# Fourier stage, last part: spectra transposed for two units at a time, into two tiles used in turn

## Chip, cores and metric

The kernel runs on one core of one Trainium2 chip. The metric is the device time of one execution in microseconds (us). Three executions of the kernel before took 6373.64, 6377.86 and 6387.61 us; the median is 6377.86 us.

## The reference

The reference is a four-layer network over an image tensor of 4 x 64 x 64 x 128 floats. Each layer is a mixing part and a feed-forward part. The change lies in the mixing part of the third layer, a Fourier neural operator with attention, and there in its last part. Cut to what is computed in that part (`p` is the spectral convolution of the attention's output, whose half-spectrum the kernel holds on chip when the part begins):

```python
        p = _fno_layer(av, Pcw, Psw, H, W)
        a = _inorm(p + xa, attn_w, attn_b)
        an = _inorm(a, norm2_w, norm2_b)
        m = _fno_layer(an, m0cw, m0sw, H, W, inner_norm=True, act=True)
        m = _fno_layer(m, m1cw, m1sw, H, W, inner_norm=True, act=False)
        out = _inorm(m, mon_w, mon_b) + a
```

with `_fno_layer` being an inverse Fourier transform of a filtered spectrum plus a pointwise skip, `_inorm` a normalization over an image, and everything in float32.

## The kernel before

**Units.** The last part handles 16 units: four batches `b`, four groups `g` each. A unit is a generator, `group(b, g, pT)` at L2187, with 28 steps between its yields. It takes the half-spectrum of its 16 images, brings it back to the image (`inverse` at L2049, with the matmuls of L2200 and L2066), normalizes, transforms forward (`transform` at L2071, `spectra` at L2085), multiplies with the first filter on VectorE (`filtered` at L2094, instructions of L2101 and L2106), brings it back (`back` at L2111, matmuls of L2116), applies the activation (L2173), and repeats this with the second filter.

**Rounds.** Units are run as a software pipeline. In one round each active unit does two steps. Every fourth round a new unit enters, and a unit lives 14 rounds, so that three to four units are active in each. Within a round the units are taken in an order by their age. The order on each engine comes out of a scheduler that mostly keeps the order in which instructions are written, and brings forward what is ready when an engine would be idle.

**The spectra.** The half-spectrum lies in the SBUF tile `ph`, 128 x 2 x 64 x 66: the partitions are images of two batches, 64 rows each. The first inverse needs it with the 66 frequencies on partitions, in the tile `pT`. `groups()` at L2280 makes it for a whole batch when the batch's first unit is due: eight PSUM tiles `ptp` of 66 x 8 x 64, each filled by eight TensorE transposes with 64 partitions in (L2287) and each copied to `pT` by one ScalarE copy (L2288). `pT` has one buffer; a batch's four units read it. This falls at the start of rounds 0, 16, 32 and 48.

**PSUM banks.** The tiles of tag `pr` take turns in three PSUM banks: the `prf` of `transform`, the `pz` of `spectra`, the `pi` of `inverse`, and also the `ptp` of the transposes. `pf` has four banks and `pm` one. A `pr` bank comes free when ScalarE (`fr` at L2081, `ir` at L2059, `pT` at L2288) or VectorE (`w` at L2101, for `pz`) has read it.

**Warming.** `warm` at L2044 puts matmuls whose result is overwritten (L2047) ahead of some real ones, so that TensorE is busy there.

Where a new unit enters, TensorE's order is: the second half of `prf` of the unit that is in its seventh stage (L2079), the transposes if a batch begins (L2287), the new unit's `pi` (L2200), then warming and the back transform of the unit of stage 4 (L2047, L2116), then `pz` of the unit of stage 8 (L2090). ScalarE's order at that place is: the activation `m` and `fr` of the stage-7 unit, six of its `sk` (L2173), the `pT` copies if a batch begins, and the new unit's `ir`.

Of the kernel before, what the change touches and what calls it, by code (L numbers as in the profile page):

```python
# [10 lines left out]
F32 = mybir.dt.float32  # L11
# [1576 lines left out]
def stage_fourier(k, a):  # L1588
# [11 lines left out]
    nc, tc = k.nc, k.tc  # L1600
    with ExitStack() as octx:
# [55 lines left out]
        with ExitStack() as ctx:  # L1657
# [8 lines left out]
            with ExitStack() as ctx2:  # L1666
# [3 lines left out]
                ps = ctx2.enter_context(tc.tile_pool(name="fo_ps", bufs=2, space=PSUM))  # L1670
# [94 lines left out]
                for b in range(4):  # L1765
# [4 lines left out]
                    for g in range(8):  # L1770
# [5 lines left out]
                        for hf in range(2):  # L1776
                            pr = ps.tile([128, 2, 256], F32, tag="pr", name="pr")
# [70 lines left out]
            with ExitStack() as ctx2:  # L1848
                yp = ctx2.enter_context(tc.tile_pool(name="fo_y", bufs=3))
                ps = ctx2.enter_context(tc.tile_pool(name="fo_pss", bufs=2, space=PSUM))  # L1850
                for hg in range(4):
                    hs = slice(8 * hg, 8 * hg + 8)
                    acc = [ps.tile([128, 8, 64], F32, tag=f"acc{bp}", name=f"acc{bp}") for bp in range(2)]
                    for g in range(17):
                        n = 128 if g < 16 else 64
# [31 lines left out]
        ph = php.tile([128, 2, 64, 66], F32, tag="ph", name="ph")  # L1887
        with ExitStack() as ctx:
# [15 lines left out]
            with ExitStack() as ctx2:  # L1904
                sm = ctx2.enter_context(tc.tile_pool(name="fo_as", bufs=2))
                ps = ctx2.enter_context(tc.tile_pool(name="fo_psa", bufs=2, space=PSUM))
# [8 lines left out]
                for bp in range(2):  # L1915
                    for q in range(4):
                        pt = ps.tile([128, 4, 128], F32, tag="pt", name="pt")
# [7 lines left out]
                for bp in range(2):  # L1925
                    pt = ps.tile([128, 128], F32, tag="pt", name="pta")
# [20 lines left out]
            with ExitStack() as ctx2:  # L1947
# [4 lines left out]
                ps = ctx2.enter_context(tc.tile_pool(name="fo_psv", bufs=3, space=PSUM))  # L1952
# [20 lines left out]
                for q in range(16):  # L1973
                    acc = [ps.tile([128, 3, 132], F32, tag="acc", name=f"acc{bp}") for bp in range(2)]
                    for hp in range(16):
                        n = 2 * q + hp // 8
# [37 lines left out]
        with ExitStack() as ctx:  # L2014
            bp_ = ctx.enter_context(tc.tile_pool(name="fo_b", bufs=1))
            sm = ctx.enter_context(tc.tile_pool(name="fo_m", bufs=2))
            ps = ctx.enter_context(tc.tile_pool(name="fo_psm", bufs=3, space=PSUM))
            mw = []
            for i in range(2):
# [3 lines left out]
                for u in range(2):  # L2023
                    p, n = mc[:, 2 * u], mc[:, 2 * u + 1]
# [127 lines left out]
            def inv(d):  # L2152
                r = eight("r")
                nc.vector.reciprocal(r, d)
                return r
# [31 lines left out]
            def group(b, g, pT):  # L2187
# [7 lines left out]
                    nc.gpsimd.tensor_tensor(sk[:, h4], sk[:, h4], xa[:, h4], op=ALU.add)  # L2195

                def terms(out, h, j):
                    n0 = 16 * g + 8 * h + 2 * j
                    for a in range(2):
                        nc.tensor.matmul(  # L2200
                            out[64 * a : 64 * a + 64], pT[:, a, n0 : n0 + 2, :].rearrange("p n y -> p (n y)"), ra[:, a, :], start=True, stop=True
                        )

                pfs = yield from inverse(terms, dya)
                for h in range(2):
                    h4 = slice(4 * h, 4 * h + 4)
# [32 lines left out]
                r, q, c, bias = inv(d), eight("q"), eight("c"), eight("sh")  # L2239
# [4 lines left out]
                y = tile8("m", 4)  # L2244
# [19 lines left out]
                r, q = inv(d), eight("q")  # L2264
# [12 lines left out]
                yield  # L2277
                yield

            def groups():  # L2280
                for b in range(4):
                    pT = bp_.tile([66, 2, 64, 32], F32, tag="pT", name="pT")
                    rows = slice(64 * (b % 2), 64 * (b % 2) + 64)
                    for q in range(8):
                        pt = ps.tile([66, 8, 64], F32, tag="pr", name="ptp")
                        for j in range(8):
                            nc.tensor.transpose(pt[:, j, :], ph[rows, b // 2, 8 * q + j, :], k.ident[rows, rows])  # L2287
                        nc.scalar.copy(pT[:, q // 4, :, 8 * (q % 4) : 8 * (q % 4) + 8].rearrange("p n y -> p y n"), pt)  # L2288
                    for g in range(4):
                        yield group(b, g, pT)  # L2290

            waiting, active, rounds = groups(), [], 0
            while waiting is not None or active:
                n = next(waiting, None) if waiting is not None and rounds % 4 == 0 else None
                if n is not None:
                    active.insert(0, [n, 0])
                elif rounds % 4 == 0:
                    waiting = None
                active.sort(key=lambda a_: {13: 0, 7: 12}.get(a_[1], a_[1]))
                for _ in range(2):  # L2300
                    for a_ in active:
                        next(a_[0])
                for a_ in active:
                    a_[1] += 1
                active = [a_ for a_ in active if a_[1] < 14]
                rounds += 1
# [736 lines left out]
def body(nc, tc, x, out, parts):  # L3043
    with ExitStack() as ctx:
        k = Ctx(nc, tc, ctx)
        dram = ctx.enter_context(tc.tile_pool(name="x1", bufs=1, space=DRAM))
        x1 = dram.tile([4, 64, 64, 128], F32, tag="x1", name="x1")
        stage_deformable(k, x, x1, *parts["conv0"].values())
        k.load_x(x1, ctx)
        stage_expert_choice(k, *parts["ffn0"].values())  # L3050
        stage_triangle(k, *parts["conv1"].values())
        stage_recurrent(k, *parts["ffn1"].values())
        stage_fourier(k, {n[3:]: v for n, v in parts["conv2"].items()})
        stage_moe(k, *parts["ffn2"].values(), "L2")
        stage_pair_attention(k, *parts["conv3"].values())
        stage_moe(k, *parts["ffn3"].values(), "L3")
        k.store_x(out)
# [25 lines left out]
```

## Time and profile before

| | |
|---|---|
| median of three executions | 6377.86 us |
| profiled execution, its own time | 6364.91 us |
| its span | 6363.0 us |
| mean granted TensorE clock | 0.906 |
| PE busy over the span | 5519.0 us (87%) |
| DVE busy | 4620.7 us (73%) |
| ACT busy | 2911.1 us (46%) |
| the transposes L2287 | x256, first at 3240.8, last at 3702.7 us |
| the copies L2288 | x32, median 1076 ns |
| the matmuls L2200 | x512, first at 3250.8, last at 3818.4 us |

The table is read like this: the part in question runs from about 3240 to 3960 us of the span. PE is TensorE's matmul row, PEld its weight loads, DVE is VectorE, ACT is ScalarE, POOL is GpSimd. The granted clock is the share of full TensorE speed that the chip allowed; it changes within the part. A line such as L2200 is a line of the kernel before.

### The profile page before, as it was taken

Reading aid. Unit: us, or ns where it says so; the run is one execution under the profiler, and the core shown is the slowest. Engines: PE = TensorE matmul, PEld = TensorE weight load, DVE = VectorE, ACT = ScalarE, POOL = GpSimd, SP = SyncE. Lnnn points to the kernel's source line nnn. Section 1 sums busy time; section 2 is a strip of 40 time slices with the busy share of each in tenths; the row PEclk is TensorE's granted clock in tenths of the full one; section 3 lists DMA queues with packets and bytes.
Section 4 is the critical chain, followed back from the end, with each engine's and each line's share of the span. In section 5 each row is a group of like instructions: output and inputs, shape, how many; then the busy total and the mean of one; then the engine's idle time right before and its main releaser. Section 6 shows DMA issues by size and latency. Waiting matters only on the chain. (4 is left out here: it accounts for less than half of the span.)

```text
span 6363.0 us, 143766 instructions
## 1 busy us (share of the span) xinstructions
PE 5519.0 (87%) x57327; PEld 2980.4 (47%) x57327; DVE 4620.7 (73%) x9921; ACT 2911.1 (46%) x6599; POOL 2075.5 (33%) x1828
## 2 busy tenths in 40 slices
PE   8978888856688788988999987988998998989999
PEld 4446666644456564333455654335234253252233
DVE  7868777745377753868978888875866857858877
ACT  5635555533154332750145554755344353353375
POOL 0012222210001111007841111443645654636545
PEclk9988888987789899999998997997997988979999
DMA  6666888871500013039920000002111112111101
GB/s 171 178 183 203 244 244 241 248 228 37 176 1 1 2 39 84 11 106 190 182 59 12 13 11 6 1 7 62 37 51 44 40 40 53 39 53 43 32 20 33
DMA packets 714227, 545.15 MB, mean 86 GB/s; under 512 B 299872, under 2 KB 625000, under 8 KB 710216
## 3 DMA queue, kind: packets, MB, share of 16 engines
q1 hardware_dynamic: 671400, 495.22, 29.1%
q10 hardware_dynamic: 42144, 40.58, 2.0%
q8 instruction: 458, 7.50, 0.5%
q14 instruction: 225, 1.84, 0.1%
HBM read 366.25 MB, written 152.86 MB: 82 GB/s over the span
## 5 line engine op out<-in xcount | busy, mean ns | idle before, releaser
L2901 DVE TENSOR_TENSOR t<-S,q 128x1536 f32<-128x1536 f32 x512 | 893.5, 1754 | 165.1 <-PE S L2901 165.1
L2901 POOL TENSOR_TENSOR t<-t,q 128x512 f32<-128x512 f32 x512 | 652.0, 1273 | 509.1 <-ACT t L2901 504.3
L2901 ACT COPY t<-S 128x512 f32<-128x512 f32 x512 | 300.2, 586 | 836.4 <-PE S L2901 763.3
L2901 PE MATMUL S<-R,L 32*128 32x512 f32 x4096 | 611.8, 651 | 53.9 <-DMA R<-wd 42.0
L2901 PE MATMUL acc<-t,sum 128*32 128x512 f32 x4096 | 548.3, 608 | 0.6 <-DVE t L2901 0.5
L2567 PE MATMUL pe<-ew,yT 128*128 128x512 f32 x1024 | 490.7, 615 | 27.3 <-DVE xs L2573 24.8
L937 DVE COPY_PREDICATED band<-bit,band 128x384 f32<-128x384 int32 (+11 forms) x384 | 313.5, 928 | 168.0 <-ACT band L928 148.7
L918 PE MATMUL S<-kpad,qm 32*64 32x144 f32 (+3 forms) x8192 | 358.3, 399 | 70.8 <-ACT band L928 26.5
L2573 DVE SCALAR_TENSOR_TENSOR xs<-pe,gate,xs 128x128 f32<-128x128 f32 x1024 | 331.2, 344 | 96.6 <-PE pe L2567 81.7
L2901 PEld LDWEIGHTS S<-R,L 32*128 32x128 f32 x4096 | 178.7, 186 | 472.2 <-ACT t L2901 396.9
L1989 PE MATMUL acc<-w,attT 128*64 128x396 f32 x2048 | 347.9, 499 | 25.9 <-issue 15.1
L2576 ACT ACTIVATE sc<-pe,gate 128x128 f32<-128x128 f32 x1024 | 291.2, 379 | 161.6 <-PE pe L2567 139.8
L1985 DVE TENSOR_TENSOR w<-xp,e 128x1188 f32<-128x1188 f32 x256 | 335.9, 1385 | 33.2 <-ACT xp L1968 15.9
L918 PEld LDWEIGHTS S<-kpad,qm 32*64 32x64 f32 x8192 | 262.0, 149 | 125.8 <-issue 60.8
L1029 PE MATMUL pt<-ident,D 128*128 128x128 f32 x1536 | 259.5, 316 | 62.6 <-DMA D<-dd 45.7
L2567 PEld LDWEIGHTS pe<-ew,yT 128*128 128x128 f32 x1024 | 183.5, 194 | 267.7 <-issue 172.3
L1984 POOL TENSOR_TENSOR w<-xtl,e 128x396 f32<-128x396 f32 x256 | 260.7, 1035 | 117.1 <-DMA e<-ed 74.2
L1031 ACT COPY dt<-pt 128x512 f32<-128x512 f32 x384 | 204.2, 594 | 133.6 <-PE pt L1029 132.8
L2901 PEld LDWEIGHTS acc<-t,sum 128*32 128x32 f32 x4096 | 81.3, 108 | 392.2 <-issue 366.7
L1445 POOL TENSOR_TENSOR xs<-xs,zT 128x512 f32<-128x512 f32 x32 | 39.6, 1281 | 677.3 <-DVE zT L1444 676.8
L1989 PEld LDWEIGHTS acc<-w,attT 128*64 128x64 f32 x2048 | 158.2, 137 | 215.7 <-issue 145.3
L1029 PEld LDWEIGHTS pt<-ident,D 128*128 128x128 f32 x1536 | 212.8, 203 | 85.6 <-DMA D<-dd 58.5
(544 smaller groups left out, 11691.6 us busy)
## 6 DMA issues: line engine op xcount, KB each, us to landing
vb<-vd SPq DMA_DIRECT2D x272, 256.0 KB
e<-ed SPq DMA_DIRECT2D x64, 792.0 KB
D<-dd SPq DMA_DIRECT2D x128, 192.0 KB
D<-dd SPq DMA_DIRECT2D x128, 168.0 KB
D<-dd SPq DMA_DIRECT2D x128, 144.0 KB
w<-in_e_weight_dram ACTq DMA_DIRECT2D x16, 1024.0 KB
w<-in_e_weight_dram SPq DMA_DIRECT2D x16, 1024.0 KB
D<-dd SPq DMA_DIRECT2D x128, 120.0 KB
```

Source lines behind the costliest of these rows:

```text
L918: ins = nc.tensor.matmul(acc[g][64 * h : 64 * h + 64].rearrange("p (a s) c -> p a s c", a=3), qm[rows, h, m, :], keys, start=(m == 0), sto ...
L937: nc.vector.copy_predicated(flat[:, :, 0:n], bit[:, 0, :, i : i + 1].to_broadcast([128, 48, n]), flat[:, :, s : s + n])
L1029: ins = nc.tensor.transpose(pt[:, g, :], D[:, g, ty : ty + 382 : 3], k.ident)
L1031: nc.scalar.copy(dt, pt)
L1445: nc.gpsimd.tensor_tensor(k.xs[b][:, 4 * g : 4 * g + 4, :], k.xs[b][:, 4 * g : 4 * g + 4, :], s, op=ALU.add)
L1984: nc.gpsimd.tensor_tensor(w[:, 3:4], planes[q][:, 3:4], wide(1, [[132, 3], [1, 132]]), op=ALU.mult)
L1985: nc.vector.tensor_tensor(w[:, 0:3].rearrange("p b c m -> p b (c m)"), xp[:, q % 2], wide(3, [[1, 396]]), op=ALU.mult)
L1989: nc.tensor.matmul(acc[b // 2][64 * (b % 2) : 64 * (b % 2) + 64].rearrange("p c m -> p (c m)"), attT[:, b // 2, hp, 64 * (b % 2) : 64 * (b ...
L2567: nc.tensor.matmul(pe[h].rearrange("p e c -> p (e c)"), yT[:, 128 * t : 128 * t + 128], ew[:, 4 * h : 4 * h + 4, :].rearrange("p e c -> p ...
L2573: nc.vector.scalar_tensor_tensor(xt, pe[0][:, e, :], gate[:, t, e : e + 1], xt, op0=ALU.mult, op1=ALU.add)
L2576: nc.scalar.activation(sc[:, e, j, :], pe[1][:, e, :], AF.Copy, scale=gate[:, t, 4 + e : 5 + e])
L2901: last[engine] = f(*args, **kw)
```

## The change

The transposes are no longer made for a batch of 64 partitions when it begins, but for a pair of units, of 32 partitions. `turned(p, a)` makes half of pair `p`: for one half `a` of the rows it fills two PSUM tiles of 66 x 16 x 32, by 16 transposes of 32 partitions each, and copies each with one ScalarE copy. Both halves of the first pair are made before the loop. From then on one call stands at the end of every fourth round, 14 in all, so that a pair is ready before its first unit enters. `pT` is half as large, 66 x 2 x 32 x 32, and has two buffers in turn. The units read it with an offset for the unit's place in the pair. The list of waiting units is replaced by a count, and the order within a round is given by a table `rank`.

```diff
                 def terms(out, h, j):
-                    n0 = 16 * g + 8 * h + 2 * j
+                    n0 = 16 * (g % 2) + 8 * h + 2 * j
...
-            def groups():
-                for b in range(4):
-                    pT = bp_.tile([66, 2, 64, 32], F32, tag="pT", name="pT")
-                    rows = slice(64 * (b % 2), 64 * (b % 2) + 64)
-                    for q in range(8):
-                        pt = ps.tile([66, 8, 64], F32, tag="pr", name="ptp")
-                        for j in range(8):
-                            nc.tensor.transpose(pt[:, j, :], ph[rows, b // 2, 8 * q + j, :], k.ident[rows, rows])
-                        nc.scalar.copy(pT[:, q // 4, :, 8 * (q % 4) : 8 * (q % 4) + 8].rearrange("p n y -> p y n"), pt)
-                    for g in range(4):
-                        yield group(b, g, pT)
-
-            waiting, active, rounds = groups(), [], 0
-            while waiting is not None or active:
-                n = next(waiting, None) if waiting is not None and rounds % 4 == 0 else None
-                if n is not None:
-                    active.insert(0, [n, 0])
-                elif rounds % 4 == 0:
-                    waiting = None
-                active.sort(key=lambda a_: {13: 0, 7: 12}.get(a_[1], a_[1]))
+            pTs = {}
+
+            def turned(p, a):
+
+                if a == 0:
+                    pTs[p] = bp_.tile([66, 2, 32, 32], F32, tag="pT", name="pT", bufs=2)
+                b, r0 = p // 2, 64 * (p // 2 % 2) + 32 * (p % 2)
+                rows = slice(r0, r0 + 32)
+                for y0 in (0, 16):
+                    pt = ps.tile([66, 16, 32], F32, tag="pr", name="ptp")
+                    for j in range(16):
+                        nc.tensor.transpose(pt[:, j, :], ph[rows, b // 2, 32 * a + y0 + j, :], k.ident[rows, rows])
+                    nc.scalar.copy(pTs[p][:, a, :, y0 : y0 + 16].rearrange("p n y -> p y n"), pt)
+
+            for a in range(2):
+                turned(0, a)
+            rank = {n: i for of in ((0, 4, 8, 12), (13, 1, 5, 9), (2, 6, 10), (3, 11, 7)) for i, n in enumerate(of)}
+            active, rounds = [], 0
+            while rounds < 64 or active:
+                n = rounds // 4
+                if rounds % 4 == 0 and n < 16:
+                    active.append([group(n // 4, n % 4, pTs[n // 2]), 0])
+                active.sort(key=lambda a_: rank[a_[1]])
                 for _ in range(2):
                     for a_ in active:
                         next(a_[0])
+                if rounds % 4 == 3 and n < 14:
+                    turned(n // 2 + 1, n % 2)
                 for a_ in active:
                     a_[1] += 1
                 active = [a_ for a_ in active if a_[1] < 14]
```

## The prediction

> **What bounds it now.** The chain of waits that ended last lies in the last stages and says nothing of this part, so I read the part itself: first where the transposes run (instructions of L2287, L2288), then the timelines of TensorE and ScalarE at a place where a batch begins and at one where only a unit enters, then the granted clock there. Where only a unit enters, TensorE shows this (start, length, engine, line, operation, out<-in, count, and the idle time before it with its releaser):
>
> ```profile
> 3449.97 1.64 PE L2079 MATMUL prf<-dyp,m 128*128 128x128 f32 x8 [0.50 <-ACT m L2173]
> 3453.14 1.16 PE L2079 MATMUL prf<-dyp,m 128*128 128x128 f32 x8 [1.36 <-ACT fr L2081]
> 3454.23 1.09 PE L2200 MATMUL pi<-ra,pT 66*64 66x128 f32 x16
> 3455.62 1.09 PE L2200 MATMUL pi<-ra,pT 66*64 66x128 f32 x16 [0.30 <-ACT fr L2081]
> 3458.60 4.33 PE L2047 MATMUL pi<-ph,ident 128*128 128x512 f32 x6 [1.88 <-ACT ir L2059]
> 3462.77 3.73 PE L2116 MATMUL pi<-rx,w 66*128 66x128 f32 x32
> 3466.34 1.88 PE L2090 MATMUL pz<-fr,fwp 128*66 128x512 f32 x4
> ```
>
> and ScalarE this:
>
> ```profile
> 3455.67 2.40 ACT L2173 ACTIVATE sk<-sk,sh,s 128x128 f32<-128x128 f32 x6
> 3457.98 1.05 ACT L2059 COPY ir<-pi 128x512 f32<-128x512 f32 x2
> ```
>
> I call this stretch, 3450 to 3458.6, the hole. TensorE waits in it four times, each time for a `pr` bank or an input that ScalarE holds, and the last wait decides: L2047 needs the bank that the first `ir` frees, and that stands behind six `sk`. VectorE then waits for `pz` (it idles 1.42 us ahead of its L2101 at 3467.40). So the cycle runs through ScalarE in the hole, TensorE from L2047 to `pz`, VectorE and TensorE together, and back.
>
> The first L2047 of this kind starts at 3298.05 for unit 2, then at 3334.32, 3383.13, 3420.93, 3458.60, 3496.20, 3544.47, 3581.81, 3621.26, 3659.46, 3707.95, 3745.47, 3782.99 and 3820.54 for unit 15: 522.5 us for 13 periods. A plain period is 37.55 us; the three in which a batch begins are 48.8, 48.3 and 48.5. In the first of these TensorE and ScalarE show:
>
> ```profile
> 3368.66 1.91 PE L2287 MATMUL ptp<-ident,ph 64*66 64x64 f32 x16
> 3372.90 5.33 PE L2287 MATMUL ptp<-ident,ph 64*66 64x64 f32 x48 [2.33 <-ACT pT L2288]
> 3378.16 1.17 PE L2200 MATMUL pi<-ra,pT 66*64 66x128 f32 x4
> 3379.53 3.67 PE L2200 MATMUL pi<-ra,pT 66*64 66x128 f32 x28 [0.19 <-ACT pT L2288]
> 3383.13 4.52 PE L2047 MATMUL pi<-ph,ident 128*128 128x512 f32 x6
> ```
>
> ```profile
> 3369.51 2.40 ACT L2173 ACTIVATE sk<-sk,sh,s 128x128 f32<-128x128 f32 x6
> 3371.82 1.91 ACT L2288 COPY pT<-ptp 66x512 f32<-66x512 f32 x2
> ...
> 3374.00 5.47 ACT L2288 COPY pT<-ptp 66x512 f32<-66x512 f32 x6 [0.18 <-PE ptp L2287]
> ```
>
> Two tiles are transposed at once; the third waits for a bank, until the six `sk` and one copy are through. In the next rows each is a stretch: its ends and length, then busy time of PE, PEld, DVE, ACT and POOL with counts, the granted clock, the DMA share and GB/s:
>
> ```profile
> 3366.06:3386.54 20.48, 17.36 (x108) 13.91 (x109) 13.43 (x41) 16.83 (x32) 5.94 (x4) 0.50 0.09 27
> ...
> 3458.22:3461.64 3.42, 3.04 (x4) 1.49 (x5) 3.42 (x11) 1.11 (x3) 1.20 (x1) 0.50 0.14 43
> ```
>
> The clock is halved for the whole burst although TensorE is busy in 17.36 of 20.48 us, so neither transposes nor L2200 keep it up; in a plain hole it is half for one stretch of 3.41 us and full for the 34.13 us around it. All changes of the clock lie on one grid of that step, and 37.55 is eleven steps: the period is tied to it.
>
> **What is removed.** The three bursts: 145.6 us less three plain periods of 37.55 is 32.9 us. The start too: of eight copies four remain ahead of unit 0. There the 46 transposes from 3245.74 wait for GpSimd's `ph`, and the last copy ends at 3252.14. With four tiles, two of them free of that wait, some four copies at 0.9 (six took 5.41) go: 3.6, say 4 us. It could be nothing, if unit 0's `sk` (GpSimd, 3254.81 to 3256.07) holds instead; I keep 0 to 5.
>
> **What is added.** The transposes double to 512, in 14 calls of 32 plus 64 at the start. One pair of load and matmul took 5.33/48 = 111 ns at half clock (17 in 1.14 us, some 60 ns, at full clock, at 3240.85). With half as many columns moving and the same 66-column load, a transpose takes between half and all of that: 32 of them cost 1.0 to 3.6 us. I take 2. Up to 3.4 us they lie in waits of TensorE that are there anyway (0.30 + 1.88) or in time that the next point takes, so they add nothing themselves; were that cover gone, 1 to 3.6 us a call. Their copies have the old size, 66x512, and stride: 1.08 us each, two a call.
>
> [...]
>
> **What is moved, and the new wait.** The call stands where the burst stood: behind the stage-7 `prf`, ahead of the new unit's L2200. On TensorE all that follows is queued behind it: L2200, L2047, L2116, `pz`; VectorE waits for the last. There are three `pr` banks. Now L2200 starts at 3454.23 in the two that are free or nearly so. In the new order the two `ptp` take these two, and the third holds `pz` until VectorE's L2101 ends at 3458.59. So L2200 starts when the first `pT` copy is through, or with the third bank. In the burst that copy stands behind the six `sk`; there it would run from 3457.98 to 3459.06. The second bank follows 0.9 later. L2200 then takes 16 + 16 matmuls, 2.2 us at full clock (the rows above: two of 1.09) or 32 x 3.67/28 = 4.2 at half clock. The clock is half from 3458.22 on, so I take 4.2. L2047 starts at 3459.06 + 4.2 = 3463.26 in place of 3458.60: 4.7 us later, with 2.7 as the low end, and zero if the banks come free otherwise. A gain in a plain hole is excluded, since nothing is taken out of it. SP's `sk` transfers and GpSimd's adds keep their order; the transfers of a unit land well ahead.
>
> **The period.** From L2047 to `pz` TensorE takes 6.2 us plus half the time Y in which the clock is still half: 3458.60 to 3466.34 is 7.74 with Y = 3.04, 3581.81 to 3591.07 is 9.26 with Y = 6.12. From `pz` to the next L2047 it is 29.87 (3466.34 to 3496.20, 3428.73 to 3458.60). So a plain period is 29.87 + 6.2 + 1.5 = 37.6, and a new one 36.07 + 4.7 + Y/2. Y was between 2.50 (3544.47 to 3546.97) and 6.12; the later start falls in the middle of a grid step, which sometimes counts as busy and sometimes not. I take Y = 3.1 and a period of 42.3; ends 38.8 + 1.5 = 40.3 and 43.8.
>
> **The sum.** Twelve periods end in a hole with a call (units 3 to 14) and one, unit 15's, does not: 12 x 42.3 + 37.55 - 522.5 = +22.7 us. Calls at units 1 and 2, where the pipeline is still filling: 1 to 4 us each, together +5. The start: -4. In all +24 us. On the profiled execution's 6364.9 that is 6389; the median shown lies 13 us above it, so I forecast 6377.9 + 24 = **6402 us**, slower.
>
> **Rivals.**
> - *The holes hide it.* The transposes are short, TensorE waits 3.7 us in a hole, and ScalarE idles 5 us soon after. If the scheduler orders banks so that L2200 still starts by 3456, all periods are 37.55: 13 x 37.55 - 522.5 = -34, with the start -38: **6340 us**, faster; with a period of 39.2, -17. The burst's rows speak against it: there too the third tile waited for ScalarE, and the copies stood behind `sk`.
> - *One grid step.* L2200 runs at full clock or in the third bank: 2.7 us later, and the period locks at twelve steps, 40.96: 12 x 40.96 + 37.55 - 522.5 + 1 = +8, **6386 us**, which can't be told from no change.
> - *Two steps.* The busy share of a step falls short, as after 3581.81 (clock 0.50 for two steps), in most periods: 44.4, +49, **6427 us**. These rows speak for it:
>
> ```profile
> 3581.10:3584.50 3.40, 2.69 (x3) 1.18 (x4) 3.40 (x11) 1.44 (x4) 1.35 (x2) 0.50 0.08 25
> 3584.50:3587.90 3.40, 3.40 (x8) 1.81 (x7) 3.40 (x17) 0.00 (x0) 1.50 (x2) 0.50 0.46 132
> ```
>
> - *It does not reorder.* `rank` gives the same order in each round as the old key, so no other effect is to come from it.
>
> **Chances.** Forecast 0.42, two steps 0.14, one step 0.19, hidden 0.25. Changes within 0.2%, 13 us, are about what a measurement of this kernel can't tell from none. Slower 0.57, same 0.18, faster 0.25. The likeliest's own range is 6390 to 6416; the range reaches to hidden and two steps, 6348 to 6428, and leaves out about a tenth at either end.
>
> **What would show it.** Right: in the plain holes L2200 idles for `pT` L2288 or for `pz`'s bank and starts some 4.5 us later behind the `prf`; L2047 to L2047 is 41 to 44 us in twelve periods and 37.5 in the last; the bursts of 10 us at half clock are gone; the start ends near 4 us sooner. Wrong: L2200 follows the transposes without a wait, or the copies of `pT` go ahead of `sk`, or the period stays at 37.55.

## The result and the profile after

The changed kernel took 6405.53 us (median of 4 runs, 6395.6 to 6417.98) against 6375.75 us of the kernel before (4 runs beside it, 6370.3 to 6387.61): a ratio of 1.0051, 95% interval 1.0036 to 1.0066, so slower by 30 us, where the forecast was 6402 us. The profiled execution took 6395.6 us with a span of 6393.8 us, 30.8 us more than the span before. By stretches, each measured between the same instructions in both traces:

| stretch | before | after | difference |
|---|---|---|---|
| start of the span to the first transpose | 3240.85 | 3241.43 | +0.6 |
| first transpose to L2047 of unit 1's entry | 28.67 | 29.29 | +0.6 |
| unit 1 to unit 2 | 28.53 | 33.86 | +5.3 |
| unit 2 to unit 15, 13 periods | 522.49 | 549.09 | +26.6 |
| unit 15 to the end of the span | 2542.46 | 2540.13 | -2.3 |

No period is a burst any more, and none of the twelve with a call is plain. L2047 starts at 3304.58 for unit 2, then at 3345.10, 3388.09, 3431.23, 3473.84, 3516.46, 3559.12, 3601.75, 3644.43, 3687.06, 3729.78, 3772.42, 3815.09 and 3853.67: 42.54 us on average for the twelve (42.61 to 42.71 once it has settled), 38.58 for the last. TensorE's timeline of the changed kernel where an odd unit, the fifth, enters (L2291 is the line of its transposes, L2292 that of their copies):

```profile
3421.37 2.08 PE L2079 MATMUL prf<-dyp,m 128*128 128x128 f32 x8 [1.36 <-ACT fr L2081]
3423.38 2.02 PE L2291 MATMUL ptp<-ident,ph 32*66 32x32 f32 x32
3427.62 3.68 PE L2200 MATMUL pi<-ra,pT 66*64 66x128 f32 x32 [2.23 <-ACT pT L2292]
3431.23 4.39 PE L2047 MATMUL pi<-ph,ident 128*128 128x512 f32 x6
3435.46 3.73 PE L2116 MATMUL pi<-rx,w 66*128 66x128 f32 x32
3439.03 1.88 PE L2090 MATMUL pz<-fr,fwp 128*66 128x512 f32 x4
```

and ScalarE's at the same place:

```profile
3424.22 2.40 ACT L2173 ACTIVATE sk<-sk,sh,s 128x128 f32<-128x128 f32 x6
3426.53 1.93 ACT L2292 COPY pT<-ptp 66x512 f32<-66x512 f32 x2
```

The six `sk` come first, then the two copies. The first copy ends at 3427.57, and 0.05 us later L2200 starts, after 2.23 us of waiting. From the second half of L2079 to L2047 it is now 9.86 us; in the plain hole before it was 5.46 (3453.14 to 3458.60). The next hole, of the sixth unit, shows one thing more:

```profile
3463.43 1.16 PE L2079 MATMUL prf<-dyp,m 128*128 128x128 f32 x8 [1.36 <-ACT fr L2081]
...
3469.35 4.55 PE L2200 MATMUL pi<-ra,pT 66*64 66x128 f32 x32 [2.33 <-ACT pT L2292]
3473.84 5.27 PE L2047 MATMUL pi<-ph,ident 128*128 128x512 f32 x6
```

L2200 again starts as the first copy ends (3469.30), but its 32 matmuls take 4.55 us in place of 3.68. Every even unit from the fourth to the fourteenth is like this, and every odd one from the third to the thirteenth has 3.68. What is late next is VectorE, which waits for `pz` (1.42 us in the hole shown before):

```profile
3440.09 1.29 DVE L2101 TENSOR_TENSOR w<-pz,f 66x512 f32<-66x512 f32 x2 [6.08 <-PE pz L2090]
```

The granted clock is half for 10.24 or 13.65 us in each of these holes, where the plain hole shown before had 3.41. Rows of stretches, with busy time of PE, PEld, DVE, ACT and POOL, then the clock:

```profile
3420.72:3434.37 13.65, 10.77 (x76) 8.46 (x77) 12.36 (x41) 8.76 (x18) 5.21 (x4) 0.50 0.14 40
3434.37:3465.10 30.73, 28.86 (x157) 18.84 (x155) 24.43 (x83) 17.09 (x38) 3.31 (x3) 1.00 0.00 1
```

### The profile page after: what moved, and what is told of

Its sections match the earlier page's. It is cut to its first block, busy times and chain, and to the rows that moved or that the text cites. A ratio compares the mean times of both kernels' runs of the same rounds, so it can differ in the third digit from the quotient of the medians.

```text
span 6393.8 us, 144287 instructions
## 1 busy us (share of the span) xinstructions
PE 5526.4 (86%) x57583; PEld 2982.4 (47%) x57583; DVE 4617.9 (72%) x9921; ACT 2912.4 (46%) x6599; POOL 2076.2 (32%) x1828
## 5 line engine op out<-in xcount | busy, mean ns | idle before, releaser
L918 PE MATMUL S<-kpad,qm 32*64 32x240 f32 (+3 forms) x8192 | 352.2, 394 | 77.3 <-ACT band L928 33.8
L1445 POOL TENSOR_TENSOR xs<-xs,zT 128x512 f32<-128x512 f32 x32 | 39.5, 1269 | 669.0 <-DVE zT L1444 668.6
```

The costliest lines, as they stand in the source:

```text
L918: ins = nc.tensor.matmul(acc[g][64 * h : 64 * h + 64].rearrange("p (a s) c -> p a s c", a=3), qm[rows, h, m, :], keys, start=(m == 0), sto ...
L1445: nc.gpsimd.tensor_tensor(k.xs[b][:, 4 * g : 4 * g + 4, :], k.xs[b][:, 4 * g : 4 * g + 4, :], s, op=ALU.add)
```

## The experiments

The theory was that of the prediction: the two `ptp` tiles take the `pr` banks that L2200 had, L2200 waits for a copy that stands behind six `sk`, and all that follows is late. The rivals: the place of the call on ScalarE, the transposes themselves (their time and the clock), and, in the last two runs made, a wait for data. The runs are grouped here by what they take away and not by the order in which they were made, so some expectations name a run that stands further down. Each run is read by its average period (L2047 to L2047 at entering units, taken between units 4 and 13, where all have settled, over whole repeats of the run's pattern, so that long and short periods count alike; 42.7 us in the change), by the distance from unit 1's L2047 to unit 15's, and by its time. The kernel before took 6369.66 to 6377.36 us beside them. Where a time is of one run, it is the profiled one.

**What all calls cost.** The 14 calls are left out; ahead of the loop the first pair is made as in the change.

```diff
-                    active.append([group(n // 4, n % 4, pTs[n // 2]), 0])
+                    active.append([group(n // 4, n % 4, pTs[0]), 0])
...
-                if rounds % 4 == 3 and n < 14:
-                    turned(n // 2 + 1, n % 2)
```

> The changed kernel without the 14 calls in the loop: all units read the first pair's spectra, so 14 units compute with other data; transposes and copies of the loop are left out. All theories: every period is plain, 37.5 us, and from unit 2 to unit 15 it is 488 us; the kernel is 33 to 40 us faster than the one before. It gives the floor, and what is left of the difference to the kernel before at units 0 to 2 is the start's.

6326.41 us (one run), 47.8 us below the kernel before where 33 to 40 were expected; by the spans of the profiled executions it is 38.4. Unit 1 to 15 takes 513.8 us, where the change has 583.0 and the kernel before 551.0. The period settles at 37.55. From the first transpose to unit 1's L2047 it is 25.04 us, 3.6 less than before. So all that the calls cost between units 1 and 15 is 69.2 us; the kernel before lies 37.2 us over the same floor, 32.9 of them in its three bursts.

**The transposes alone.** The calls stay, without their copies; as in the run before, all units read the first pair's spectra.

```diff
...
-                    nc.scalar.copy(pTs[p][:, a, :, y0 : y0 + 16].rearrange("p n y -> p y n"), pt)
+                    if p == 0:
+                        nc.scalar.copy(pTs[p][:, a, :, y0 : y0 + 16].rearrange("p n y -> p y n"), pt)
...
-                    active.append([group(n // 4, n % 4, pTs[n // 2]), 0])
+                    active.append([group(n // 4, n % 4, pTs[0]), 0])
```

> The changed kernel with the loop's 448 transposes in place but their copies to pT left out (units read the first pair's spectra). Theory (banks): a bank is free again as soon as its 16 transposes are through, L2200 follows without a wait for ScalarE, and the period is 37.5 to 38.5. Rival (the transposes themselves): TensorE has all their work at the same place, so the period stays above 41. Rival (clock: transposes do not keep it up, so the hole is longer at half speed): 39 to 41.

6360.17 us; 545.5 us; periods of 38.9, 41.2, 41.1 and 39.3 in turn, 40.1 on average. TensorE's timeline of this kernel:

```profile
3453.07 2.28 PE L2291 MATMUL ptp<-ident,ph 32*66 32x32 f32 x32
3455.28 3.68 PE L2200 MATMUL pi<-ra,pT 66*64 66x128 f32 x32
3458.89 5.38 PE L2047 MATMUL pi<-ph,ident 128*128 128x512 f32 x6
```

From the transposes to L2047 nothing waits here, and yet 31.7 of the 69.2 us are spent: transposes, L2200 and L2047 stand one behind another on TensorE, most of it at half clock (the granted clock is 0.52 on average from 3450 to 3460 us). The theory's 37.5 to 38.5 us was missed, and so was the 41 and more of the transposes' rival; the clock's rival, 39 to 41, covers it. This is what the prediction priced as the transposes with their cover gone: 2.5 us a period.

**The place ahead of the `sk`.** The call is written between the two steps of the last round, so that its copies go ahead of five of the six `sk`.

```diff
-                for _ in range(2):
+                for i in range(2):
...
-                if rounds % 4 == 3 and n < 14:
-                    turned(n // 2 + 1, n % 2)
+                    if i == 0 and rounds % 4 == 3 and n < 14:
+                        turned(n // 2 + 1, n % 2)
```

> The changed kernel with the call moved between the two steps of the fourth round, so that the copies of pT go ahead of five of the six sk on ScalarE; banks as in the changed kernel. Theory (banks): the first copy ends some 2.4 us sooner behind the prf, L2200 starts that much sooner, and L2047 then waits for ir behind the sk: about 2 us a period more than the plain 37.55 in place of 5.1, so 39.5 to 41.0. Rival (the transposes themselves): 42 to 43 as in the changed kernel. Rival (ScalarE's time for the copies): ScalarE has the same work ahead of ir, so 42 to 43 as well.

6367.46 us; 556.5 us; 40.9 on average, within what the theory said. The place behind the activation is worth 1.7 us a period. The periods are 41.4 to 42.4 for even units from the sixth on and 39.4 to 40.1 for odd ones, of which the theory says nothing: in the even holes L2200 stops once more for a copy and takes 4.87 us in place of 3.68. The runs on banks and data below say what it waits for.

**Other banks.** The transposes go to the four buffers of `pf`; the place is that of the change.

```diff
-                    pt = ps.tile([66, 16, 32], F32, tag="pr", name="ptp")
+                    pt = ps.tile([66, 16, 32], F32, tag="pf", name="ptp", bufs=4)
```

> The changed kernel with its transposed tiles in the four banks of tag pf instead of the three of tag pr; work and place are the same. Theory (banks): in the changed kernel the new unit's L2200 waits for the first pT copy because the two transposed tiles hold the pr banks, and the copies stand behind six sk. Without that L2200 follows its prf at once, and only the two copies (1.9 us) stay ahead of ir: L2047 to L2047 39.5, or 41.0 if it locks to the clock's steps, against 42.64 in the changed kernel; the whole 16 to 38 us faster than the changed kernel, within 15 us of the kernel before. Rival (the transposes themselves: twice as many, 32-row loads, on TensorE): the period stays at 42 to 43 and the time at that of the changed kernel. Rival (ScalarE's time for the copies alone): two copies are 1.9 us, so 39.5 too, but L2200's start would not matter.

6386.24 us (median of 10 runs), ratio 1.0022, interval 1.0012 to 1.0032; 568.3 us. The time is 19 us below that of the changed kernel, as expected, but the period is not: odd units have 38.2 to 38.5 us and even ones 45.0 to 45.7 (up to the L2047 that follows the last L2200), 41.8 on average where 39.5 or 41.0 was said. In the even holes L2047 stands between two parts of L2200, and waits:

```profile
3462.03 0.43 PE L2200 MATMUL pi<-ra,pT 66*64 66x128 f32 x2 [0.32 <-ACT fr L2081]
3466.72 2.08 PE L2047 MATMUL pi<-ph,ident 128*128 128x512 f32 x2 [4.26 <-DVE w L2101]
3468.73 3.68 PE L2200 MATMUL pi<-ra,pT 66*64 66x128 f32 x28
```

At first sight this is a fault of the order. So the order was fixed: the same kernel, with L2047 of the back transform tied behind the new unit's L2200.

```diff
...
+                with tc.issue_after(entered[0].ins) if n == 3 and entered[0] is not None else ExitStack():
+                    for _ in range(n):
...
-                        nc.tensor.matmul(
+                        entered[0] = nc.tensor.matmul(
```

> As the run with the transposes in the pf buffers at the change's own place, but with L2047 of the back transform tied behind the new unit's last L2200, so that no hole is in the other order. TensorE's order is then that of the run with the call behind L2200 and the pf buffers; ScalarE's differs from it in one thing: the two pT copies (1.9 us) stand ahead of the new unit's ir and not behind. Theory (the banks put L2200 on the activation, and of the rest the copies count because they stand ahead of ir): L2200 doesn't wait for a pT copy; L2047 waits for ir, which comes 1.9 us later than in that run: 38.3 + 1.9 = 40.2 us a period, or 40.96 if it locks at twelve steps of the clock; unit 1 to unit 15 in 545 to 558 us, the whole 6355 to 6372 us. Rival (the copies are hidden at this place too): 37.55 to 38.6 us a period, 6335 to 6345 us. Rival (the banks were not what mattered): 42 us or more, 6390 us or more.

6395.07 us; 582.3 us: missed by 23 us. What came is the price of the last rival, 42.7 us a period on average. The odd units have 40.3 us, near the 40.2 that were expected, and the even ones 45.0. TensorE's timeline, an odd unit's hole and an even one's:

```profile
3501.18 1.97 PE L2203 MATMUL pi<-ra,pT 66*64 66x128 f32 x32 [0.18 <-DVE w L2104]
3506.62 5.49 PE L2050 MATMUL pi<-ph,ident 128*128 128x512 f32 x6 [3.48 <-DVE w L2104]
...
3542.94 1.49 PE L2203 MATMUL pi<-ra,pT 66*64 66x128 f32 x4
3548.05 3.67 PE L2203 MATMUL pi<-ra,pT 66*64 66x128 f32 x28 [3.62 <-ACT pT L2295]
3551.66 5.34 PE L2050 MATMUL pi<-ph,ident 128*128 128x512 f32 x6
```

(L2203 is L2200 here, L2050 L2047, L2104 L2101, L2062 the copy `ir` and L2295 the copy `pT`.) VectorE's last L2104 ahead of the odd hole's L2050, and ScalarE's `ir`:

```profile
3505.89 0.68 DVE L2104 TENSOR_TENSOR w<-pz,f 66x512 f32<-66x512 f32 x1
3506.88 1.05 ACT L2062 COPY ir<-pi 128x512 f32<-128x512 f32 x2
```

So in the odd hole L2050 does not wait for `ir`, as the theory had it: it starts 0.05 us after VectorE has read `pz`, and `ir` is copied later. That the 40.3 us agree is luck. In the even hole L2203 has its bank and still waits for the copies. The call ahead of an even unit makes the second half of the pair that begins with this very unit, and L2200 reads both halves: it waits for data. The prediction had not looked at which half each call makes.

**Banks and data apart.** So each call makes the half that is needed one unit later, first with the `pr` banks of the change, then with `pf`.

```diff
-            for a in range(2):
-                turned(0, a)
+            for q in range(3):
+                turned(q // 2, q % 2)
...
-                if rounds % 4 == 3 and n < 14:
-                    turned(n // 2 + 1, n % 2)
+                if rounds % 4 == 3 and n < 13:
+                    turned((n + 3) // 2, (n + 1) % 2)
```

> As the changed kernel, banks and place alike, but each call makes the half that is needed one unit later (three halves ahead of the loop, 13 calls in it). In the change every second call makes the second half of the very pair whose first unit enters next, so that this unit's L2200 needs both copies as data, and not only a bank; here no L2200 reads what the call ahead of it has made. The order of the instructions on TensorE and ScalarE is the same. Theory of the prediction (the two pr banks): L2200 still starts when the first pT copy is through, in every hole, 42 us or nearly that a period, or 40.96 where the 0.9 us less in every second hole loses a step of the clock; unit 1 to unit 15 in 560 to 583 us, the whole 6382 to 6405 us. Rival (the data, not the banks): L2200 follows the transposes without a wait, 37.55 to 40 us a period, 6365 us or less.

6400.2 us; 569.7 us; 42.1 us on average. An even unit's hole on TensorE, the eighth's:

```profile
3559.46 1.11 PE L2291 MATMUL ptp<-ident,ph 32*66 32x32 f32 x16 [0.41 <-ACT fr L2081]
3562.89 3.68 PE L2200 MATMUL pi<-ra,pT 66*64 66x128 f32 x32 [2.32 <-ACT pT L2292]
```

No L2200 needs the copy's data here, and it still waits 2.32 us for a copy: the bank. Its length is 3.68 us in even units too.

> Both at the change's own place: the transposes in the pf buffers and each call one unit earlier, so that L2200 waits for the copies neither by banks nor by data. The copies still stand ahead of the new unit's ir. Theory: no hole has L2200 waiting for pT, the 45-us holes of the two runs with the pf buffers at this place are gone, L2047 is 1.6 us later than in the run with the call behind L2200 (5.4 in place of 3.9 us from L2200 to L2047): 39.1 us a period, or 40.96 where that locks at twelve steps; unit 1 to unit 15 in 530 to 555 us, the whole 6342 to 6372 us. Rival (the slow holes came from the order of L2047 and the banks of pz): 42 us or more on average, 6385 us or more.

6357.97 us; 541.4 us; 39.3 to 40.1 us from the fourth unit to the thirteenth, odd and even alike, 39.8 on average. What TensorE waited for ahead of L2200 in this kernel (us, times) names no copy any more:

```profile
  ACT fr L2081: 5.3, 7
  DVE w L2101: 4.5, 16
  DVE v L2261: 0.7, 3
```

What is left of the wait lies ahead of L2047 (the last row is ScalarE's):

```profile
3529.20 1.97 PE L2200 MATMUL pi<-ra,pT 66*64 66x128 f32 x32 [0.18 <-DVE w L2101]
3534.64 5.49 PE L2047 MATMUL pi<-ph,ident 128*128 128x512 f32 x6 [3.47 <-DVE w L2101]
...
3534.90 1.05 ACT L2059 COPY ir<-pi 128x512 f32<-128x512 f32 x2
```

From L2200 to L2047 it is 5.44 us, as expected, and the period lies between the 39.1 and the 40.96 us that were said. But here too L2047 starts when VectorE has read `pz`, ahead of `ir`, which stands behind the two copies.

The kernels with the call at the change's place, in us a period, so make a square:

| | second half just ahead of its unit | one unit earlier |
|---|---|---|
| `pr` banks | 42.7 (the change) | 42.1 |
| `pf` banks | 41.8, with L2047 tied 42.7 | 39.8 |

Taking away the wait for data alone brings 0.6 us, that for the bank alone 0.8, or nothing with L2047 tied; both together bring 2.9. The bank holds L2200 in every hole, so without the data's wait it still does. The data hold it in the even holes only: with the banks gone and L2047 tied, the odd periods are 2.3 us shorter than in the change and the even ones 2.4 longer. Why the even ones grow by as much as the odd ones lose is not shown.

**Behind the new unit's L2200.** The call is written into the first step of the entering unit, right behind its L2200, so that each half is made more than three rounds earlier than in the change, and no L2200 behind it needs it at once. First with the `pr` banks.

```diff
-                for _ in range(2):
+                for i in range(2):
...
-                if rounds % 4 == 3 and n < 14:
-                    turned(n // 2 + 1, n % 2)
+                        if i == 0 and a_[1] == 0 and n < 14:
+                            turned(n // 2 + 1, n % 2)
```

> The changed kernel with the call moved behind the new unit's L2200 (its first step), still in the pr banks; on ScalarE the copies then stand behind the two ir. Theory (banks): L2200 is no longer delayed, but the 32 transposes stand ahead of L2047 and need banks that VectorE (L2101) and ir free at 58.5 on the scale of the plain hole, so they and the slower clock put L2047 back by 2 to 3.5 us: period 39.5 to 41.0. Rival (the transposes themselves): 41 to 43. Rival (ScalarE's time for the copies): the copies are out of the way, so 37.55.

6364.7 us; 552.3 us; the period runs into 40.96, as far as the theory's range goes, and stays there to the thirteenth unit. TensorE's timeline:

```profile
3491.18 3.68 PE L2200 MATMUL pi<-ra,pT 66*64 66x128 f32 x32
3494.96 2.02 PE L2291 MATMUL ptp<-ident,ph 32*66 32x32 f32 x32
3496.91 5.49 PE L2047 MATMUL pi<-ph,ident 128*128 128x512 f32 x6
```

The waits are gone, and the transposes now stand ahead of L2047. With the `pf` buffers as well (both edits):

> The changed kernel with the call behind the new unit's L2200 and the transposed tiles in the banks of tag pf. The transposes then fill TensorE's wait for the activation, ahead of the second half of prf, and the copies stand behind ir where ScalarE idles. Theory (banks and place on ScalarE): nothing is on the cycle any more, all periods 37.55, unit 2 to unit 15 in 488 us; 30 to 38 us faster than the kernel before, 60 us faster than the changed kernel. Rival (the transposes themselves): 40 or more a period, no faster than the kernel before. Rival (clock): 39 to 41.

6340.48 us (median of 6 runs), ratio to the kernel before 0.995, interval 0.9936 to 0.9963: faster than both kernels. Unit 1 to 15 takes 526.2 us, the period is 37.7 to 40.2, 38.4 on average, where 37.55 was expected. TensorE and then ScalarE, where the eighth unit enters:

```profile
3518.98 0.81 PE L2291 MATMUL ptp<-ident,ph 32*66 32x32 f32 x18
...
3521.77 1.97 PE L2200 MATMUL pi<-ra,pT 66*64 66x128 f32 x32 [0.18 <-DVE w L2101]
3525.63 4.26 PE L2047 MATMUL pi<-ph,ident 128*128 128x512 f32 x6 [1.90 <-ACT ir L2059]
```

```profile
3525.02 1.04 ACT L2059 COPY ir<-pi 128x512 f32<-128x512 f32 x2
...
3527.47 1.92 ACT L2292 COPY pT<-ptp 66x512 f32<-66x512 f32 x2
```

With banks of their own the transposes need not wait for the place they are written at: the scheduler has put them between the matmuls of L2079, ahead of L2200 and here at full clock (L2079's eight matmuls behind them take 1.16 us, where they took 2.08 at half clock in the change), where TensorE waits for the activation. The copies stand behind `ir`. L2047 waits for `ir` as in a plain hole before. The longer periods, 39.0 to 40.2 us, are those of units 4, 6, 10 and 14: there the clock is half for 10.24 us and L2200 takes 3.68 us.

**The transposes held behind L2200.** As that run, but tied behind the last L2200, into TensorE's wait of 1.9 us for `ir`.

```diff
...
+                    with tc.issue_after(entered[0].ins) if entered[0] is not None else ExitStack():
+                        for j in range(16):
...
```

> As the run with the call behind the new unit's L2200 and its banks among the pf buffers, but with the 32 transposes tied behind the last L2200, so that all of them stand in TensorE's wait for the copy ir (1.9 us in that run) and none between the two halves of L2079. They need 1.1 us at full clock or 2.2 us at half clock. Theory (what counts is whether a transpose stands ahead of the hole's end): L2047 is delayed by 0 to 0.4 us, period 37.55 to 38.0 us, unit 1 to unit 15 in 514 to 522 us (526 in that run), the whole 33 to 40 us faster than the kernel before. Rival (the clock's windows: L2047 begins so late in a window of 3.413 us that a delay of some tenths loses it): holes with 6.8 and 10.2 us of half clock in turn, 38.5 us or more a period, no faster than that run. Rival (transposes cost their own time wherever they stand): 39.5 us or more.

6373.4 us (median of 12 runs), ratio 1.0001, interval 0.9989 to 1.0012; 552.5 us; 40.96 from the fourth unit to the thirteenth. The theory missed. TensorE's timeline at the third unit and at the seventh:

```profile
3339.61 1.56 PE L2292 MATMUL ptp<-ident,ph 32*66 32x32 f32 x32
3341.57 5.49 PE L2047 MATMUL pi<-ph,ident 128*128 128x512 f32 x6 [0.39 <-ACT ir L2059]
...
3503.51 2.01 PE L2292 MATMUL ptp<-ident,ph 32*66 32x32 f32 x32
3505.45 5.49 PE L2047 MATMUL pi<-ph,ident 128*128 128x512 f32 x6
```

At the third unit the transposes still fit into the wait, but the clock stays half for two steps (6.83 us). From the next hole on it is half from L2079 to the start of L2116 (13.65 us), L2200 takes 3.68 us, and `ir`, whose first copy starts at 3503.05, is done before the transposes are: now they delay L2047. The rival with a fixed price per call fits the period, that of the clock only in part, since it expected long and short holes in turn. Whether the same kernel would keep 37.6 us if the part began at another point of the clock's grid was not tried.

## Why the prediction was right

- *The bursts, -32.9.* They are gone as said. The floor without calls is 37.55 us a period, as the prediction took it.
- *The start, -4.* 3.6 by the run without calls.
- *The transposes, 2 us a call, hidden.* 2.02 us at half clock, and in the change TensorE waits 2.2 us more behind them, so they add nothing there. The price with the cover gone, 1 to 3.6, was met by the run without copies: 2.5 a period. This cover is the wait that the change itself brings, so taking that wait away alone did not bring the period back to 37.55. The pace was measured: from one transpose's start to the next it was at half clock, by the median, 107 ns with 64 rows (the kernel before) and 57 ns with 32 (the change), and at full clock 56 and 35 ns; the 66 columns loaded were the same. The moving columns were halved with the rows, so this is the pace of a pair and not that of its load alone.
- *The new wait.* Shown: L2200 starts as the first copy ends, in every hole with a call from the third unit on, and the run that takes only the data away keeps the wait of 2.32 us for the bank. L2047 comes 4.4 us (fifth unit) and 5.0 us (sixth) later behind L2079 than in the plain hole; 4.7 was said. Part of that agreement is luck: the 4.2 us for L2200 at half clock were scaled up from a row of 28 matmuls, and all 32 take 3.68 where only the bank is waited for and 4.55 where the data are too, 4.1 on average. What was not seen: for every even unit the second copy is also data, 0.9 us more of L2200. The run with each half one unit earlier puts that at 0.6 us a period on average.
- *The clock.* The prediction took half clock to begin with L2200; in the change it begins, from the fourth unit's hole on, ahead of the transposes or with the second half of them, and lasts 10.24 or 13.65 us. That "the bursts of 10 us at half clock are gone" was wrong: there is one in each hole now. It cost little beyond the sum, since L2200 at half clock and half of Y were in it.
- *The period, 42.3.* 42.54. With 38.58 for the last in place of 37.55 it makes +26.6 us where +22.7 stood.
- *The ramp.* This is the term that was mis-sized. The start and the calls at units 1 and 2 were to be -4 + 5 = +1 us and measured 0.6 + 5.3 = +5.9. The start gave its 3.6 us; against the run without calls, unit 1's call cost 4.2 us and unit 2's 7.0, where 1 to 4 each was said. Unit 2 is even: its L2200 starts at 3296.61, but the last copy ends at 3300.93. In the run with each half one unit earlier the distance from unit 1 to unit 2 is 31.63 in place of 33.86 us.
- *The end.* -2.3 us behind unit 15, of which nothing was said; the runs do not explain it. The same stretch takes 2545.9 us in the run without calls, so it differs by some microseconds from trace to trace.

The sum was +24 us on the profiled execution, and +30.8 were measured: 3.9 of the difference from the periods, 4.9 from the ramp, 0.6 ahead of the part, and -2.3 at the end, with -0.3 of rounding in the sum. Two figures of the prediction do not follow from its own: its period ends of 40.3 and 43.8 us give 6378 to 6420 us by its sum, not 6390 to 6416, and the four waits in its rows of the hole add to 4.0 us, not 3.7.

Of the rivals, "the holes hide it" came near to true in another kernel: 6340 us was its price, and 6340.48 us is the time with the banks, the data and the place all changed. That the two agree so closely is luck: its periods were to be 37.55 us and are 38.4, and from unit 2 to unit 15 the profiled execution gains 24.5 us on the kernel before, where the price had 34. One step of the grid is what the runs with the transposes ahead of L2047 gave. Periods of 44.4 us on average were not seen. That the new order changes nothing holds as far as the run without calls shows it: its plain period is the old one.

## What to carry to other kernels

Before a step is moved to a regular place, ask three things of it there: whose buffers it takes, who reads its result next, and what stands ahead of its last instruction on its engine. Here the bank alone and the data alone each kept the period at 41.8 to 42.7 us, against 42.7 with both, so an experiment that took away only one of them showed 0 to 0.8 us of the 2.9 that both together bring. And when the new unit's wait was gone, the next one, for `pz` or `ir`, decided. Work that is needed a period later can be written behind the entering unit's own first instruction, into buffers that nobody on the critical cycle waits for, if TensorE stays free to do it earlier: 38.4 us a period so, and 40.96 where it was held behind that instruction.

## What was not expected of the hardware

In this part the cycle did not lengthen by just what was added to it: in eight of the kernels here it fell into patterns that repeat after a whole number of the clock's steps. A step is 3.413 us: in the traces of the kernel before and of the change each stretch of the part at one clock lasts a whole number of it, as 3.41 us in a plain hole before, 20.48 (six) in a burst and 13.65 (four) in the fifth unit's hole of the change. One period is 11 steps (37.55 us) without calls and 12 (40.96) in two of the runs; two periods are 25 steps in the change (42.64 + 42.67 = 85.31 us, 25 steps are 85.33) and in the run with the order tied (45.03 + 40.30); three are 35 in the run with both waits taken away and 37 in the one that takes away only the data; four are 47 in the run without copies (160.42 us).

What a step needs so that the next is granted at full clock stays open. In the traces of the kernels before and after, from 3290 to 3870 us, the steps at full clock with less than 2.0 us of busy TensorE were all followed by half clock and those with more than 2.6 us all by full; in between both came. Of the steps at half clock none with less than 2.8 us was followed by full, as the step from 3581.10 with 2.69 was not, but some that were busy throughout were not either. Of two steps with the same busy time of TensorE, one in the run with the transposes held behind L2200 and one in the kernel before, the first was followed by half clock and the second by full:

```profile
3371.09:3374.51 3.42, 2.04 (x11) 1.42 (x10) 3.42 (x16) 3.41 (x10) 0.00 (x0) 1.00 0.00 0
3374.51:3377.92 3.41, 2.93 (x18) 2.71 (x20) 3.41 (x11) 3.17 (x7) 0.00 (x0) 0.50 0.03 7
```

```profile
3451.40:3454.80 3.40, 2.04 (x22) 1.79 (x23) 3.40 (x11) 3.37 (x8) 0.00 (x0) 1.00 0.00 0
3454.81:3458.22 3.41, 1.61 (x26) 1.12 (x22) 3.41 (x8) 3.41 (x10) 1.41 (x2) 1.00 0.01 2
```
